# A two-layer graph attention kernel: the additive mask built by GpSimd during batch entry 0, and three moves in the hand-written order (seam transposes, queries, row normalization)

## The chip, the cores and the metric

One Trainium2 chip, one core of it. The metric is device time in microseconds (us) of one execution of the whole program; lower is better. Before the change it is 4377.3 us, the median of three runs (4373.14, 4377.3 and 4388.37).

## What is computed

The input `x` is 8 batch entries of 2048 nodes with 256 features, fp32; `adj` is one 2048 x 2048 int32 adjacency, shared by all entries. Two layers, each with a residual and a layer norm:

```
def _L0_gnn_ref(x, adj, prior, W, a_src, a_dst, beta_tilde, W_out):
    x_proj = jnp.einsum('bnd,hdf->bhnf', x, W)                 # 8 heads of 32
    e = leaky_relu(e_src[..., :, None] + e_dst[..., None, :], ALPHA)
    e = e + (beta * jnp.log(prior + EPS))[:, None, :, :]       # prior is adj
    e = jnp.where(adj > 0, e, neg_inf)
    h = softmax(e) @ x_proj ;  return h @ W_out.T
def _L1_gnn_ref(inp, adj, W1, W2, W3):
    e = leaky_relu((inp @ W1) @ (inp @ W2).T, ALPHA)
    e = jnp.where(adj > 0, e, NEG_INF)
    return relu(softmax(e) @ (inp @ W3))
x = _layernorm(x + _L0_gnn_ref(...)) ;  x = _layernorm(x + _L1_gnn_ref(...))
```

The mask of layer 1 (`where(adj > 0, e, NEG_INF)`) is applied as an addition: a bf16 tile `pen` is 0 where there is an edge and -3.0e38 where there is none.

## The kernel before

**Stages.** Layer 0 (class `Gat`, with `Unit` for one pair of heads and one half of the 2048 rows) is handled for batch entry 0 by itself: 4 head pairs x 16 steps, `g0.step(k)`, from the start to about 512 us. This stage is laid out by a scheduler, except on TensorE (PE), whose order is that of the program text. Its first 16 steps also make the matrix m = (adj + eps)^beta, masked: `make_m` (L199 to L209) loads an int32 block `adj_t` of 128 x 2048 (L203), and DVE (L205, L208) and ACT (L206, L207) turn it into `m`; TensorE transposes it and the result is stored in DRAM as `mt_d` (L214 to L222). All later uses load `mt_d` (L224). The projections of entries 1 to 7 are also interleaved with this stage.

From there on the order on all engines is written out by hand: `Stream` (L589) feeds the tiles of layer 0 of entry b while `Dot` (L666) does layer 1 of entry b-1. Its calls are `ahead` (ACT scales a tile, L478; DVE combines it, L492; GpSimd adds it up, L498) and `eat` (TensorE's products, L524). Between two entries lies a **seam** (L873 to L896): `rows(g)` (L401) projects the attention output (`y`, L409), adds the residual (L413) and takes statistics (L414); `rows_scale` (L416) computes the two layer-norm factors, `f[:,0]` on ACT (L420, L421) and `f[:,1]` = -mean * f[:,0] on DVE (L422); `rows_end` (L424) applies them on ACT (L429). `turn` (L437) then transposes the result x1 (`tr1`, L448; copied to SBUF as `x1t` by ACT, L449) and multiplies it by W3 (`h3p`, L454; copy L456). In `turn`, `lag` says how many pairs of 128-row blocks the h3 products stand behind the transposes: 1, and 4 in the last entry. At L882 to L885 the seam calls `stream.ahead(1)`, which at that place starts a new unit (two copies of `c` into PSUM on ACT, L488, and the first L492 of that unit), and then `next(turns)`.

After a seam come 16 **rows** of layer 1 (`Dot.step`, L705), each 128 nodes: scores `e` (L691), leaky relu `p` (L693), the mask and the row maximum in one DVE instruction (L700, reads `p` and `pen`), exp on ACT (L702), transposes `pt` (L718) and copies `pts` (L720), the product with h3 (`acc`, L742), relu on ACT (L743), residual `z` (L745), statistics (L747, L749). The layer norm of a row is finished one row later in `end_row` (L757): L762 and L763 give 1/std, L764 multiplies it on ACT by the negated mean (negated on DVE, L750), L765 scales `z`; then `store_row` stores it. Every fourth row `queries` (L675) makes the next four rows' left factor `h1` (`h1p`, L680; copies L682); it stands at the head of that row's step, ahead of its transposes. TensorE's small results share two PSUM buffers (`mm`).

**The mask.** `mask` (L229): for the rows of entry 0's layer 1 (it runs in the first streamed period, together with layer 0 of entry 1) the adjacency is loaded again, two int32 tiles `adj_r` of 128 x 1024 for each row (L237); DVE turns them into `pen` (L241), which is used and also stored in `pen_d` (L242). All later entries load `pen` from `pen_d` (L233).

The last entry's layer 1 (4069 us to the end) runs alone, with GpSimd idle.

Of the kernel before, what the change touches and what calls it, by code (L numbers as in the profile page):

```python
# [11 lines left out]
I32 = mybir.dt.int32  # L12
# [15 lines left out]
def kernel(  # L28
# [56 lines left out]
    def mm_tile(name):  # L85
        tag = banks[0]
        banks.append(banks.pop(0))
        if tag == "mm":
            return ps.tile([P, BK], F32, tag="mm", name=name)
        return pacc.tile([P, BK], F32, tag=tag, name=name)  # L90
# [7 lines left out]
    def ring_tile(name, shape=(P, N)):  # L98


        return wide.tile(list(shape), F32, tag="s", name=name, bufs=9)
# [97 lines left out]
    def make_m(n):  # L199

        rh, j2 = divmod(n, J2)
        a = wide.tile([P, NT // 2, 2 * P], I32, tag="d", name="adj_t", bufs=2)
        nc.sync.dma_start(a, adj[ts(rh, HALF), ts(j2, 2 * P)].rearrange("(t p) j -> p t j", p=P))  # L203
        m = ring_tile("m", (P, NT // 2, 2 * P))
        nc.vector.tensor_scalar(m, a, 0.0, None, ALU.max)  # L205
        nc.scalar.activation(m, m, AF.Ln, bias=eps_prior)  # L206
        nc.scalar.activation(m, m, AF.Exp, scale=beta_c)  # L207
        nc.vector.scalar_tensor_tensor(m, a, 0.0, m, ALU.is_gt, ALU.mult)  # L208
        return m  # L209
# [16 lines left out]
        nc.sync.dma_start(mt, mt_d[n, :, i])  # L226
        return mt

    def mask(it, make):  # L229

        pen = wide_tile("pen", "pen", 1, BF16)
        if not make:
            nc.sync.dma_start(pen, pen_d[ts(it, P), :])  # L233
            return pen, lambda: None
        edges = [chunk.tile([P, HALF], I32, tag="ht", name="adj_r", bufs=4) for _ in range(2)]
        for s, a in enumerate(edges):
            nc.sync.dma_start(a, adj[ts(it, P), ts(s, HALF)])  # L237

        def put():
            for s, a in enumerate(edges):  # L240
                nc.vector.tensor_scalar(pen[:, ts(s, HALF)], a, 0.0, NO_EDGE, ALU.is_le, ALU.mult)  # L241
            nc.sync.dma_start(pen_d[ts(it, P), :], pen)  # L242
        return pen, put

    def row_tile(name, bufs=4):
        return small.tile([P, D], F32, tag="row", name=name, bufs=bufs)
# [14 lines left out]
    class Gat:  # L261


        def __init__(self, b):
            self.b = b
            self.ms, self.mts, self.v = [], [], {}

        def begin(self):

# [131 lines left out]
        def rows(self, g):  # L401


            self.load_rows(g + 2)
            self.st = st = small.tile([P, IG // 2, nc.vector.BN_STATS_DIM], F32, name="st4", bufs=2)
            ys = [mm_tile("y").rearrange("p (t c) -> p t c", t=2) for _ in range(IG // 2)]
            for k in range(IG):
                for kc in range(KC):
                    nc.tensor.matmul(ys[k // 2][:, k % 2, :], self.ht[kc][:, ts(g * IG + k, P)], wot[:, kc, :],  # L409
                                     start=(kc == 0), stop=(kc == KC - 1))  # L410
            for k, y in enumerate(ys):
                z = self.x1(2 * g + k)
                nc.vector.tensor_add(z, y, self.xs[g][:, ts(k, 2), :])  # L413
                nc.vector.bn_stats(st[:, k, :], z.rearrange("p t c -> p c t"))  # L414

        def rows_scale(self):  # L416

            mv = self.st.rearrange("p a (t c) -> p (a t) c", t=2)
            self.f = f = small.tile([P, 2, IG], F32, name="f4", bufs=2)
            nc.scalar.activation(f[:, 0, :], mv[:, :, 2], AF.Ln, bias=eps_ln, scale=1.0 / D)  # L420
            nc.scalar.activation(f[:, 0, :], f[:, 0, :], AF.Exp, scale=-0.5)  # L421
            nc.vector.scalar_tensor_tensor(f[:, 1, :], mv[:, :, 1], -1.0, f[:, 0, :], ALU.mult, ALU.mult)  # L422

        def rows_end(self, g):  # L424

            for k in range(IG):
                z, f = self.x1(2 * g + k // 2), self.f
                row = z[:, k % 2, :]
                nc.scalar.activation(row, row, AF.Identity, bias=f[:, 1, k:k + 1], scale=f[:, 0, k:k + 1])  # L429
                if k % 2:  # L430
                    nc.scalar.dma_start(x1_d[self.b].rearrange("(t p) d -> p t d", p=P)[:, ts(2 * g + k // 2, 2), :], z)
# [5 lines left out]
        def turn(self):  # L437


            self.x1t = x1t = whole.tile([P, KC, N], F32, tag="x1t", name="x1t")  # L440
            self.h3 = h3 = whole.tile([P, NT, D], F32, tag="h3", name="h3")
            lag = 1 if self.b + 1 < B else 4
            for j in range(NT // 2 + lag):
                if j < NT // 2:
                    t = mm_tile("tr1")
                    for kc in range(KC):
                        for i in range(2):
                            nc.tensor.transpose(t[:, ts(kc * 2 + i, P)], self.x1(j)[:, i, ts(kc, P)], ident)  # L448
                    nc.scalar.copy(x1t[:, :, ts(j, 2 * P)], t.rearrange("p (k i) -> p k i", k=KC))  # L449
                if j >= lag:  # L450
                    t = mm_tile("h3p")
                    for i in range(2):
                        for kc in range(KC):
                            nc.tensor.matmul(t[:, ts(i, D)], x1t[:, kc, ts(2 * (j - lag) + i, P)], w3s[:, kc, :],  # L454
                                             start=(kc == 0), stop=(kc == KC - 1))
                    nc.scalar.copy(h3[:, ts(j - lag, 2), :], t.rearrange("p (i c) -> p i c", i=2))  # L456
                if j > 0:
                    yield
# [207 lines left out]
    class Dot:  # L666
# [16 lines left out]

        def scores(self, it, between=lambda c: None, after=lambda c: None):

            (pen, put), p = mask(it, self.b == 0), self.p
            for c in range(NB):
                between(c)
                t = mm_tile("e")
                for kc in range(KC):  # L690
                    nc.tensor.matmul(t, self.h1[:, kc, ts(it % IG, P)], self.x1t[:, kc, ts(c, BK)],  # L691
                                     start=(kc == 0), stop=(kc == KC - 1))
                nc.scalar.activation(p[:, ts(c, BK)], t, AF.Prelu, alpha=ALPHA)  # L693
                if c == 2:
                    put()
                if c < NB - 1:
                    after(c)
            neg = small.tile([P, 1], F32, name="neg")
            den = small.tile([P, 1], F32, name="den1")
            nc.vector.tensor_tensor_reduce(p, p, pen, -1.0, FMAX, ALU.add, ALU.min, neg)  # L700
            after(NB - 1)
            nc.scalar.activation(p, p, AF.Exp, bias=neg, scale=-1.0, accum_out=den)  # L702
            self.ahead = den

        def step(self, stream, count, lead=0):  # L705
# [16 lines left out]

            behind = count
            if it + 1 < NT:
                if (it + 1) % IG == 0:
                    self.queries((it + 1) // IG)
                self.scores(it + 1, turned, lambda c: stream.feed())
                behind -= NB
            else:
                for g in range(NB):  # L730
                    turned(g)
                stream.ahead()
                lead -= 1
            rec = small.tile([P, 1], F32, name="rec1", bufs=2)
            nc.vector.reciprocal(rec, den)
            self.end_row()
            stream.ahead(2 if it + 1 == NT else 1)
            acc = mm_tile("acc")[:, 0:D]
            for g in range(NB):
                for k in range(IG):  # L740
# [6 lines left out]
            nc.vector.bn_stats(st, z)  # L747
            f = small.tile([P, 4], F32, name="f", bufs=3)
            nc.vector.bn_aggr(f[:, 0:2], st)  # L749
            nc.vector.tensor_scalar(f[:, 0:1], f[:, 0:1], -1.0, None, ALU.mult)  # L750
            self.store_row()
            self.ended = it, z, f
            stream.eat(1)
            stream.ahead(behind - (2 if it + 1 == NT else 1) + lead)
            stream.eat(behind - 1)

        def end_row(self):  # L757


            if self.ended:  # L760
                it, z, f = self.ended
                nc.scalar.activation(f[:, 2:3], f[:, 1:2], AF.Ln, bias=eps_ln)  # L762
                nc.scalar.activation(f[:, 3:4], f[:, 2:3], AF.Exp, scale=-0.5)  # L763
                nc.scalar.activation(f[:, 2:3], f[:, 3:4], AF.Identity, scale=f[:, 0:1])  # L764
                nc.scalar.activation(z, z, AF.Identity, bias=f[:, 2:3], scale=f[:, 3:4])  # L765

        def store_row(self):
# [86 lines left out]
    for b in range(1, B + 1):  # L854
# [19 lines left out]
        for g in range(NB + 2):  # L874
            if g < NB:
                gat.rows(g)
            if g == 0 and dot:
                dot.end_row()
                dot.store_row()
            if 0 < g <= NB:  # L880
                gat.rows_end(g - 1)
            stream.eat(1)  # L882
            stream.ahead(1)
            if g > 1:
                next(turns)  # L885
            if g < NB:
                gat.rows_scale()
            if g < NB + 1:
# [14 lines left out]
    dot.step(stream, 0)  # L903
    dot.step(stream, 0)
    dot.end_row()
    dot.store_row()
# [1 line left out]
_INS = ['x', 'adj', 'L0_gnn_W', 'L0_gnn_a_src', 'L0_gnn_a_dst', 'L0_gnn_beta_tilde', 'L0_gnn_W_out',  # L908
# [27 lines left out]
```

## Time and profile before

| | |
|---|---|
| median of 3 runs | 4377.3 us |
| the profiled execution: its time | 4372.4 us |
| the profiled execution: its span | 4370.6 us |
| PE, DVE, ACT, POOL busy in the span | 4126.0, 3334.9, 2905.3, 2888.3 us |
| mean granted TensorE clock | 0.979 |

How to read it: the page lists busy time by engine, then 40 slices of the span, DMA queues, the chain of work that ended last, and groups of instructions by line. PE is TensorE's matmul side, PEld its weight loads, DVE is VectorE, ACT ScalarE, POOL GpSimd, SP the engine that issues most DMAs. A busy share is an average over stages with different limits, so the windows view, which gives busy time in chosen stretches, is more useful here. Where one period of the streamed part begins and ends is read from the first `y` product (L409) of each seam: 512.5, 1058.0, 1559.6, 2063.9, 2563.5, 3072.4, 3581.3 and 4069.0 us. The first `h1p` (L680), where the rows begin, is at 579.0, 1115.3, 1617.2, 2123.2, 2623.9, 3132.7, 3641.3 and 4095.2 us.

### The profile page before, as it was taken

The page shows a single profiled execution, that of the slowest core. Times are in us where ns is not written, and L with a number is a line of the kernel's source. Part 1 is how long each engine was busy: PE and PEld are TensorE (multiplying, and loading weights), DVE is VectorE, ACT ScalarE, POOL GpSimd, SP SyncE. Part 2 cuts the span into 40 slices and gives each one's busy share as a digit, 9 for nine tenths or more (in the row PEclk, how much of TensorE's full clock was granted, in tenths as well). Part 3 has the DMA queues.
Part 4 walks back from the last instruction along what each step waited for, and adds up shares of the span by engine and source line. Part 5 has one row for each costly group of instructions (what it writes and reads, how often), then busy time and mean ns, then how long its engine had stood idle before and what let it go on. Part 6 is the DMA issues. An engine that isn't in the chain of part 4 may idle for free.

```text
span 4370.6 us, 60300 instructions
## 1 busy us (share of the span) xinstructions
PE 4126.0 (94%) x22704; PEld 2090.3 (48%) x22704; DVE 3334.9 (76%) x3278; ACT 2905.3 (66%) x4132; POOL 2888.3 (66%) x1190
## 2 busy tenths in 40 slices
PE   7899799998999999999899999999899999999999
PEld 4444344444444444445444454444444444444766
DVE  7888788988878887788777887788787787787222
ACT  6422466676677767677777776677677776776555
POOL 0000477877788887889788877888687887888000
PEclk9999999999999999999999999999999999999999
DMA  8888755666565565556556564656555565554211
GB/s 268 275 288 285 237 198 196 218 223 218 184 198 189 188 205 191 178 195 215 186 178 203 195 207 166 193 193 197 190 199 180 186 219 171 187 192 158 79 46 46
DMA packets 346437, 843.63 MB, mean 193 GB/s; under 512 B 49696, under 2 KB 166432, under 8 KB 346144
## 3 DMA queue, kind: packets, MB, share of 16 engines
q1 hardware_dynamic: 328736, 822.99, 57.4%
q10 hardware_dynamic: 17408, 16.78, 1.1%
q8 instruction: 178, 2.92, 0.3%
q14 instruction: 115, 0.94, 0.1%
HBM read 763.76 MB, written 75.37 MB: 192 GB/s over the span
## 4 chain that ended last, share of the span: by engine, by line
PE 66%; ACT 12%; DVE 9%; issue 6%; DMA 5%; POOL 1%; SPq 1%; ACTq 0%; DVEq 0%; POOLq 0%
PE e L691 18%; PE val L524 15%; PE acc L742 14%; PE den L524 6%; PE pt L718 5%; ACT s L478 5%; DVE s L492 5%; DMA mt<-mt_d 3%; PE h3p L454 3%; DVE p L700 2%; PE h1p L680 2%; ACT p L702 2%; PE y L409 2%; ACT c L488 1%; PE proj L294 1%
## 5 line engine op out<-in xcount | busy, mean ns | idle before, releaser
L498 POOL TENSOR_TENSOR sums<-sums,s 128x1024 f32<-128x1024 f32 x1008 | 2505.7, 2523 | 272.8 <-DVE s L492 271.9
L492 DVE SCALAR_TENSOR_TENSOR s<-c,re,s 128x1024 f32<-128x1024 f32 x1232 | 1500.8, 1272 | 269.9 <-ACT c L488 197.6
L478 ACT ACTIVATE s<-mt,re 128x1024 f32<-128x1024 f32 x1232 | 1339.8, 1140 | 49.9 <-DMA mt<-mt_d 38.7
L524 PE MATMUL val<-s,v 128*32 128x512 f32 x8192 | 1094.5, 607 | 30.7 <-DVE s L492 17.8
L691 PE MATMUL e<-x1t,h 128*128 128x512 f32 x2048 | 995.8, 610 | 45.9 <-ACT pts L720 30.4
L742 PE MATMUL acc<-h,pts 128*128 128x256 f32 x4096 | 918.3, 382 | 1.5 <-ACT pts L720 1.0
L742 PEld LDWEIGHTS acc<-h,pts 128*128 128x128 f32 x4096 | 770.4, 190 | 198.5 <-ACT p L693 29.3
L700 DVE CUSTOM_DVE_ANT_0 p<-p,pen 128x2048 f32<-128x2048 f32 x128 | 459.6, 3591 | 310.3 <-ACT p L693 310.1
L492 DVE SCALAR_TENSOR_TENSOR s<-c,re,mt 128x1024 f32<-128x1024 f32 x560 | 687.5, 1268 | 0.0
L498 POOL TENSOR_TENSOR sums<-s 128x1024 f32<-128x1024 f32 x112 | 291.9, 2629 | 412.4 <-DVE s L492 405.1
L693 ACT ACTIVATE p<-e 128x512 f32<-128x512 f32 x512 | 306.8, 599 | 383.4 <-PE e L691 383.4
L524 PEld LDWEIGHTS val<-s,v 128*32 128x32 f32 x8192 | 203.1, 109 | 683.2 <-issue 442.9
L691 PEld LDWEIGHTS e<-x1t,h 128*128 128x128 f32 x2048 | 356.0, 194 | 333.9 <-issue 258.9
L702 ACT ACTIVATE p<-p,neg 128x2048 f32<-128x2048 f32 x128 | 256.5, 2004 | 374.2 <-DVE neg L700 373.6
L524 PE MATMUL den<-s,re 128*32 128x512 f32 x3264 | 443.1, 594 | 0.0
L718 PEld LDWEIGHTS pt<-ident,p 128*128 128x128 f32 x2048 | 224.1, 142 | 456.0 <-ACT p L693 129.1
L718 PE MATMUL pt<-ident,p 128*128 128x128 f32 x2048 | 332.7, 287 | 73.1 <-ACT p L702 39.5
L492 DVE SCALAR_TENSOR_TENSOR s<-c_in,re,mt 128x1024 f32<-128x1024 f32 x256 | 310.2, 1277 | 51.6 <-DMA mt<-mt_d 39.5
L720 ACT COPY pts<-pt 128x512 f32<-128x512 f32 x512 | 294.5, 579 | 79.8 <-PE pt L718 79.0
L305 POOL PARTITION_ALL_REDUCE top<-top x8 | 6.6, 821 | 428.9 <-DVE top L304 412.5
L524 PEld LDWEIGHTS den<-s,re 128*32 128x32 f32 x3264 | 110.1, 110 | 244.6 <-issue 242.9
L745 DVE TENSOR_TENSOR z<-acc,x1r 128x256 f32<-128x256 f32 x128 | 54.0, 422 | 199.0 <-ACT acc L743 189.8
(96 smaller groups left out, 2493.7 us busy)
## 6 DMA issues: line engine op xcount, KB each, us to landing
mt<-mt_d SPq DMA_DIRECT2D x992, 512.0 KB
c_in<-c_d SPq DMA_DIRECT2D x64, 1024.0 KB
pen<-pen_d SPq DMA_DIRECT2D x112, 512.0 KB
xg<-in_x_dram SPq DMA_DIRECT2D x60, 512.0 KB
adj_t<-in_adj_dram SPq DMA_DIRECT2D x16, 1024.0 KB
mt_d<-mt SPq DMA_DIRECT2D x32, 512.0 KB
rb<-rec_d SPq DMA_DIRECT2D x128, 128.0 KB
x_d<-ht ACTq DMA_DIRECT2D x64, 256.0 KB
```

The costliest lines, as they stand in the source:

```text
L454: nc.tensor.matmul(t[:, ts(i, D)], x1t[:, kc, ts(2 * (j - lag) + i, P)], w3s[:, kc, :], start=(kc == 0), stop=(kc == KC - 1))
L478: nc.scalar.activation(s[:, a], mt, AF.Copy, scale=self.gat.re[:, 1, jt, h:h + 1])
L492: nc.vector.scalar_tensor_tensor(s[:, a], self.c[a], self.gat.re[:, 0, jt, h:h + 1], m, ALU.max, ALU.mult)
L498: nc.gpsimd.tensor_tensor(self.sums[:, a], of[:, a], s[:, a], ALU.add)
L524: nc.tensor.matmul(dst[ts(q, DH), :], weights[q % 2], s[:, q % 2, ts(q // 2, BK)], start=start, stop=stop)
L691: nc.tensor.matmul(t, self.h1[:, kc, ts(it % IG, P)], self.x1t[:, kc, ts(c, BK)], start=(kc == 0), stop=(kc == KC - 1))
L693: nc.scalar.activation(p[:, ts(c, BK)], t, AF.Prelu, alpha=ALPHA)
L700: nc.vector.tensor_tensor_reduce(p, p, pen, -1.0, FMAX, ALU.add, ALU.min, neg)
L702: nc.scalar.activation(p, p, AF.Exp, bias=neg, scale=-1.0, accum_out=den)
L718: nc.tensor.transpose(t[:, ts(k, P)], p[:, ts(g * IG + k, P)], ident)
L720: nc.scalar.copy(pt, t)
L742: nc.tensor.matmul(acc, pts[g][:, ts(k, P)], self.h3[:, j, :], start=(j == 0), stop=(j == NT - 1))
```

## The change

1. **Mask.** `make_m` now also makes the mask from the block it has loaded: GpSimd writes `pen_t` (128 x 2048, bf16) from `adj_t`, and SP stores it to `pen_d`. This happens 16 times, in the first 16 steps. `mask` only loads `pen`; L237, L241 and L242 are gone.
2. **Seam.** `rows_scale` no longer issues L422; `rows_factor` does, called in the next `rows` after both residual adds and ahead of their statistics (and in `rows_end`). The two adds now stand ahead of the two statistics. `next(turns)` comes ahead of `stream.ahead(1)`, and `lag` is 2 instead of 1.
3. **Queries.** `queries` is called near the end of the step before, after the first `eat` that follows `acc`, ahead of the remaining `ahead` calls.
4. **Row normalization.** L750 and L764 are gone. A new `end_mean` computes -mean/std in one DVE instruction from two SBUF operands and then issues the ACT scaling of `z`; it is called after `stream.ahead(...)`, so that ACT's scalings of the next tile stand ahead of it, and the relu (L743) stands behind it.

```diff
@@ make_m
         nc.sync.dma_start(a, adj[ts(rh, HALF), ts(j2, 2 * P)].rearrange("(t p) j -> p t j", p=P))
+        pen = wide.tile([P, NT // 2, 2 * P], BF16, tag="c", name="pen_t", bufs=1)
+        nc.gpsimd.tensor_scalar(pen, a, 0.0, NO_EDGE, ALU.is_le, ALU.mult)
+        nc.sync.dma_start(pen_d[ts(rh, HALF), ts(j2, 2 * P)].rearrange("(t p) j -> p t j", p=P), pen)
         m = ring_tile("m", (P, NT // 2, 2 * P))
@@ mask
-    def mask(it, make):
+    def mask(it):
         pen = wide_tile("pen", "pen", 1, BF16)
-        if not make:
-            nc.sync.dma_start(pen, pen_d[ts(it, P), :])
-            return pen, lambda: None
-        edges = [chunk.tile([P, HALF], I32, tag="ht", name="adj_r", bufs=4) for _ in range(2)]
-        for s, a in enumerate(edges):
-            nc.sync.dma_start(a, adj[ts(it, P), ts(s, HALF)])
-        def put():
-            for s, a in enumerate(edges):
-                nc.vector.tensor_scalar(pen[:, ts(s, HALF)], a, 0.0, NO_EDGE, ALU.is_le, ALU.mult)
-            nc.sync.dma_start(pen_d[ts(it, P), :], pen)
-        return pen, put
+        nc.sync.dma_start(pen, pen_d[ts(it, P), :])
+        return pen
@@ Gat.rows, rows_scale, rows_end, turn
                 nc.vector.tensor_add(z, y, self.xs[g][:, ts(k, 2), :])
-                nc.vector.bn_stats(st[:, k, :], z.rearrange("p t c -> p c t"))
+            self.rows_factor()
+            for k in range(len(ys)):
+                nc.vector.bn_stats(st[:, k, :], self.x1(2 * g + k).rearrange("p t c -> p c t"))
...
-            nc.vector.scalar_tensor_tensor(f[:, 1, :], mv[:, :, 1], -1.0, f[:, 0, :], ALU.mult, ALU.mult)
+        def rows_factor(self):
+            if self.mv is not None:
+                nc.vector.scalar_tensor_tensor(self.f[:, 1, :], self.mv[:, :, 1], -1.0, self.f[:, 0, :], ALU.mult, ALU.mult)
+                self.mv = None
         def rows_end(self, g):
+            self.rows_factor()
...
-            lag = 1 if self.b + 1 < B else 4
+            lag = 2 if self.b + 1 < B else 4
@@ Dot.scores: (pen, put), p = mask(it, self.b == 0), self.p  becomes  pen, p = mask(it), self.p
-                if c == 2:
-                    put()
@@ Dot.step, end_row, and the new end_mean
             if it + 1 < NT:
-                if (it + 1) % IG == 0:
-                    self.queries((it + 1) // IG)
                 self.scores(it + 1, turned, lambda c: stream.feed())
...
             stream.ahead(2 if it + 1 == NT else 1)
+            self.end_mean()
             acc = mm_tile("acc")[:, 0:D]
...
-            nc.vector.tensor_scalar(f[:, 0:1], f[:, 0:1], -1.0, None, ALU.mult)
...
             stream.eat(1)
+            if (it + 2) % IG == 0 and it + 2 < NT:
+                self.queries((it + 2) // IG)
             stream.ahead(behind - (2 if it + 1 == NT else 1) + lead)
...
-                nc.scalar.activation(f[:, 2:3], f[:, 3:4], AF.Identity, scale=f[:, 0:1])
+        def end_mean(self):
+            if self.ended:
+                it, z, f = self.ended
+                nc.vector.scalar_tensor_tensor(f[:, 2:3], f[:, 0:1], -1.0, f[:, 3:4], ALU.mult, ALU.mult)
                 nc.scalar.activation(z, z, AF.Identity, bias=f[:, 2:3], scale=f[:, 3:4])
@@ the seam loop (end_mean is also called after each other end_row)
             stream.eat(1)
-            stream.ahead(1)
             if g > 1:
                 next(turns)
+            stream.ahead(1)
```

More of the change, by code (lines that the diff above doesn't have):

```diff
@@ L265, in __init__ @@
             self.b = b
-            self.ms, self.mts, self.v = [], [], {}
+            self.ms, self.mts, self.v, self.mv = [], [], {}, None
         def begin(self):
@@ L413, in rows @@
                 nc.vector.tensor_add(z, y, self.xs[g][:, ts(k, 2), :])
-                nc.vector.bn_stats(st[:, k, :], z.rearrange("p t c -> p c t"))
+            self.rows_factor()
+            for k in range(len(ys)):
+                nc.vector.bn_stats(st[:, k, :], self.x1(2 * g + k).rearrange("p t c -> p c t"))
         def rows_scale(self):
-            mv = self.st.rearrange("p a (t c) -> p (a t) c", t=2)
+            self.mv = mv = self.st.rearrange("p a (t c) -> p (a t) c", t=2)
             self.f = f = small.tile([P, 2, IG], F32, name="f4", bufs=2)
@@ L684, in scores @@
         def scores(self, it, between=lambda c: None, after=lambda c: None):
-            (pen, put), p = mask(it, self.b == 0), self.p
+            pen, p = mask(it), self.p
             for c in range(NB):
@@ L878 @@
                 dot.end_row()
+                dot.end_mean()
                 dot.store_row()
@@ L905 @@
     dot.end_row()
+    dot.end_mean()
     dot.store_row()
```

## The prediction

> **What bounds the kernel now.** First the page: busy time by engine, and the 40 slices (one is 109 us).
>
> ```profile
> PE 4126.0 (94%) x22704; PEld 2090.3 (48%) x22704; DVE 3334.9 (76%) x3278; ACT 2905.3 (66%) x4132; POOL 2888.3 (66%) x1190
> ...
> PE   7899799998999999999899999999899999999999
> ...
> DVE  7888788988878887788777887788787787787222
> ...
> POOL 0000477877788887889788877888687887888000
> ```
>
> TensorE is near full, so only its 4370.6 - 4126.0 = 244.6 us of idle time can be won. GpSimd is idle for the first four slices. Then the windows view (us; busy us and count of PE, PEld, DVE, ACT, POOL; clock; DMA share; GB/s):
>
> ```profile
> 35.60:175.00 139.40, 119.67 (x868) 68.94 (x870) 128.23 (x99) 101.59 (x106) 0.37 (x1) 0.95 0.82 277
> ...
> 579.00:1058.00 479.00, 442.55 (x2321) 210.61 (x2320) 421.54 (x384) 325.71 (x446) 384.33 (x154) 0.97 0.65 215
> ...
> 1115.30:1559.60 444.30, 429.43 (x2322) 206.60 (x2321) 357.35 (x348) 324.62 (x441) 372.69 (x152) 0.99 0.60 192
> ```
>
> In the stretch that makes `m` (35.6 to 175) DVE, not PE, is the fullest: 128.2 of 139.4 us. Later PE bounds. The 16 rows with the masks (579 to 1058) take 479.0 us. Next, what PE waited for in one ordinary period (1559.6 to 2061):
>
> ```profile
> PE pt L718 <- ACT p L702: 6.2, 1, 6.2
> PE h3p L454 <- ACT x1t L449: 5.5, 1, 5.5
> PE e L691 <- ACT pts L720: 5.0, 1, 5.0
> ...
> PE pt L718 <- ACT h L682: 1.5, 1, 1.5
> PE e L691 <- DVE z L745: 0.9, 1, 0.9
> ```
>
> These five are 19.1 us of 21.9 idle. Last, single lines (count: shortest/median/longest ns). L700 reads two SBUF tiles: first in the last stage, where GpSimd rests, then in the six periods where it works; L422, two small SBUF operands, likewise; then L750 (one operand) and L498, GpSimd's usual instruction.
>
> ```profile
> L700 DVE CUSTOM_DVE_ANT_0 p<-p,pen x16: 2291/2292/2293, 4106.4 to 4349.7; 128x2048 f32<-128x2048 f32 x16
> L700 DVE CUSTOM_DVE_ANT_0 p<-p,pen x95: 2605/3555/7764, 1131.1 to 4032.1; 128x2048 f32<-128x2048 f32 x95
> L422 DVE SCALAR_TENSOR_TENSOR f<-st,f x4: 161/162/165, 4075.7 to 4089.0; 128x4 f32<-128x4 f32 x4
> L422 DVE SCALAR_TENSOR_TENSOR f<-st,f x28: 161/1012/3859, 526.0 to 3625.7; 128x4 f32<-128x4 f32 x28
> L750 DVE TENSOR_SCALAR f<-f x128: 153/154/155, 633.7 to 4366.2; 128x1 f32<-128x1 f32 x128
> L498 POOL TENSOR_TENSOR sums<-sums,s x1008: 2337/2380/4482, 491.7 to 4039.2; 128x1024 f32<-128x1024 f32 x168
> ```
>
> Read them together: a DVE instruction with two SBUF operands waits while GpSimd works, one with a single operand does not. In the timeline L422 at 1099.71 ends at 1101.04, just when GpSimd's instruction ends (1098.64 + 2.34). This row prices two of the four parts.
>
> **The change, part by part** (minus is time won).
>
> *A. Entry 0's rows lose the masks: -33 us.* Gone are 32 L241 (70.3 us of DVE, mean 2.23), 32 loads of `adj_r` and 16 stores with their places in SP's queue; 16 loads of `pen` come instead. The rows of the next five periods, from first `h1p` to the next seam, take 444.3, 446.7, 440.3, 448.6 and 448.6, mean 445.7. 479.0 - 445.7 = 33.3. Next late is PE itself, as there. Bounds -25 to -37.
>
> *B. Stage 0 gains 16 GpSimd instructions: +24.* No row shows this instruction. Below: a GpSimd memset writes 128 columns in 205 ns and one column in 100, so 0.82 ns a column, 1.7 us for 2048. Above: two L498, 4.8 us. I take one L498, 2.4 us: it reads 2 x 1024 elements, as many as this one. GpSimd is free, but DVE isn't: L205, L208, L326 and L492 of this stretch (here `c` lies in SBUF) are of the kind that waits, or move two elements a cycle (L205: 2048 in 1.22 us). Two of the 16 fall before 35.6, where DVE rests. 14 x 2.4 = 34; DVE's 11.2 idle us of the stretch cover that much, 22 stay, and PE, which eats what DVE makes, ends as much later. SP: 16 stores of 512 KB, 8.4 MB, 30 us at the 277 GB/s of the row, against 0.18 x 139 = 25 us of idle queues plus the 22 new ones: covered. At the start GpSimd's first mask stands ahead of L305, and a third `adj_t` load, which waits for a buffer, now ahead of the store `c_d` on the way to the first L492: +2. Bounds: 0 (GpSimd uses only gaps) to 14 x 4.8 + 2 = +69.
>
> The Trainium skill, page "GPSIMD Engine Reference", section 3.1, gives one-input loops of few operations 1.03 cycles an element at 1.2 GHz: an estimate of 1.8 us, by which B would be about +16 and the sum about -24.
>
> *C. Seven seams: -3 each, -21.* Today PE stands from 1076.47 to 1081.59, since the `x1t` copies are queued behind two `c` copies (0.98 each) and two L478 (1.1 each), and h3's first product needs them. Then it runs cold: 8 matmuls in 3.78 us instead of 1.89. Now the copies go first (1.1 us) and h3 isn't asked for yet; but the next in PE's order is the new unit's first `val`, which needs L492, which needs `c`, and `c` is 1.1 us later: L492 from 1079.1, `val` from 1080.4 and in full from 1081.6. So the wait stays and only changes its name; won is 1 us, and one h3 product (1.9 us) that moves behind the scores into the 6.2 us that PE waits for the first exp. L422 behind the adds costs nothing: it waited for ACT 14 times, 3 us each, and does so later. Bounds: -5.5, and +1 if the new wait of part E at a seam's start delays ACT's scalings.
>
> *D. Queries earlier: -12.* PE waited 13.8 us in seven periods for `h` ahead of a transpose and 3.5 ahead of scores; two `val` groups now lie in between. I take two thirds. Bounds 0 and -17.
>
> *E. `end_mean`: +26.* Per row DVE loses L750 (0.15) and gets an instruction of L422's kind. L700's rows price its wait: mean over the 112 busy rows (459.6 - 16 x 2.29) / 112 = 3.78, so 1.48 above 2.29. 112 x 1.48 = 166 us more DVE work, 24 in a period of 502 where DVE has 100 free. ACT loses L764 (0.29 x 128). Behind the waiting instruction on DVE is the residual add L745, on ACT L765 and behind it the relu, unit copies and `pts`, for which PE waits. In one row per period (the fourth) a new unit's `c` copies and four L492 (4.86 us) stand ahead of it: there DVE would reach `end_mean` at 1779.8 instead of ACT finishing `z` at 1775.0, GpSimd is in an instruction until 1781.1, the relu goes from 1778.9 to 1782.0, and PE's 5.0 us wait for `pts` grows by 3: 7 x 3 = +21. In the other rows the relu comes about 1 us later; PE wants that buffer 4.2 us after `acc`, so only long waits show: +5. Bounds 0 and +40 for the two.
>
> The Trainium skill, page "SBUF — State Buffer", section "Who interferes with whom", speaks against B and E: DVE and GpSimd share one port pair as an exclusive lock for a whole instruction, two-operand DVE instructions contend with any GpSimd instruction that reads SBUF. The rows of L422, L700 and L750 agree (161 against 1012 ns; 154 always).
>
> **Sum:** -33 + 24 - 21 - 12 + 26 = **-16 us**. On the profiled execution, 4372.4 us (span 4370.6 and 1.8 around it), that is 4356; it lies 4.9 below the median shown, on whose scale I say **4360**.
>
> **Rivals** (median scale).
> - *Cheap GpSimd, no held row:* B +13, E1 0, seams -28. -16 - 11 - 21 - 7 = -55: 4322. For it: most PE waits in the row are short. Against: the L422 row.
> - *GpSimd as the new bound of stage 0:* its instruction takes 4.8 us, two L498. B is +69, sum +29: 4406, slower. It decides from about 3.5 us (B = +40, sum 0). For: DVE at 128 of 139. Against: one operand read, not two.
> - *`end_mean` in place of the removed wait:* L745 frees one of PE's two small buffers; in the row at 1823 it ends 1.6 us ahead of need, and L422 waited up to 3.7. If half of 112 rows lose 1.2 us, +67: 4428. For: in entry 0, where DVE was late, PE waited for L745 6.4 us, not 0.9.
> - *The seam changes the name of its wait only:* C is 0: 4382, no change.
>
> **Chances.** Forecast 0.37 (0.27 faster by over 0.3%, which is 13 us and about what this measurement tells from none; 0.10 within), first rival 0.18, second 0.20, third 0.15, fourth 0.10 (0.06 within, 0.04 slower). Faster 0.45, within 0.16, slower 0.39. The range leaves out part of the third and the best of the first: 4310 to 4425; the forecast's own is 4345 to 4378.
>
> **What would show it.** A: rows of entry 0 near 446 us instead of 479. B: the start of the first seam, 512.5 now, near 537; DVE's L492 in stage 0 longer than 1.28 us; the GpSimd instruction's mean. C: PE's wait at h3p gone, one at `val` for L492 in its place, 21 us less over seven seams. D: waits for `h` gone. E: `end_mean` near 1.6 us, PE's `pts` wait in the fourth row near 8. Wrong if GpSimd's instruction is far from 2.4 us, or if DVE isn't held by it.

## The result and the profile after

The changed kernel takes **4532.1 us** (median of four runs, 4524.5 to 4534.0) against 4379.2 for the kernel before (4373.1 to 4388.4): ratio 1.0344, 95% interval 1.0322 to 1.0366. That is 151 us slower by the ratio (153 by the two medians). The forecast was 4360, its range ended at 4425, and the sign was wrong. The profiled execution spans 4532.1 us, 161.5 more than before's.

First the page of the changed kernel: busy times, and the slices of PE and GpSimd.

```profile
PE 4188.9 (92%) x22704; PEld 2097.7 (46%) x22704; DVE 3445.5 (76%) x3246; ACT 2859.4 (63%) x4004; POOL 3060.3 (68%) x1206
...
PE   5689979999899999999899999999899999999999
...
POOL 4420157888788877888788877788777886788100
```

GpSimd now works in the first slices, and there PE has holes (5, 6, 8) where it had 7, 8, 9. The windows view of the same kernel (columns as before) for the stretch that makes `m`, and for the rows of entry 0:

```profile
35.60:175.00 139.40, 85.43 (x486) 51.03 (x484) 96.80 (x49) 62.69 (x60) 74.29 (x9) 0.77 0.58 187
698.30:1150.90 452.60, 433.76 (x2330) 207.81 (x2329) 373.85 (x348) 321.83 (x429) 378.83 (x153) 0.99 0.58 190
```

In the same 139.4 us PE does 486 products instead of 868 and DVE 49 instructions instead of 99; even the transfers fall from 277 to 187 GB/s. No engine is full: this is a chain of waits. The rows of entry 0 did get shorter, 452.6 instead of 479.0.

By the first `y` of each seam the 161.5 us split without a rest: stage 0 632.3 instead of 512.5 (+119.8), the first streamed period 518.6 instead of 545.5 (-26.9), the next six periods 7 to 15 us longer each (+66.1), the rest +2.5. What PE waits for in one ordinary period (1662.8 to 2178), the longest four:

```profile
PE e L692 <- DVE z L743: 6.8, 4, 3.2
PE val L525 <- DVE s L493: 6.6, 2, 6.2
PE pt L717 <- ACT pts L719: 6.4, 4, 2.9
PE h1p L681 <- DVE z L743: 4.5, 3, 2.3
```

Before's waits for `p`, for `x1t` ahead of `h3p` and for `h` are gone; in their place stand a `val` (a product of `eat`) that waits for DVE, and two lines that wait for `z`, the residual add behind the new `end_mean`. Single lines of the changed kernel, shortest/median/longest ns:

```profile
L205 POOL TENSOR_SCALAR pen_t<-adj_t x16: 7132/8130/12387, 18.3 to 264.8; 128x2048 bf16<-128x2048 int32 x16
L769 DVE SCALAR_TENSOR_TENSOR f<-f x128: 142/2100/4733, 771.6 to 4528.1; 128x1 f32<-128x1 f32 x128
```

I had taken 2.4 us for the first and some 1.6 for the second. The second was right (mean 1.67); the first is 8.5 on average. How a slow mask holds the stage is seen in the timeline of the changed kernel, first GpSimd's, then SP's queue:

```profile
71.92 8.12 POOL L205 TENSOR_SCALAR pen_t<-adj_t 128x2048 bf16<-128x2048 int32 x1 [8.42 <-DMA adj_t<-in_adj_dram]
87.75 8.12 POOL L205 TENSOR_SCALAR pen_t<-adj_t 128x2048 bf16<-128x2048 int32 x1 [7.70 <-DMA adj_t<-in_adj_dram]
```

```profile
80.07 0.37 SPq L206 DMA_DIRECT2D pen_d<-pen_t  x1
80.76 0.38 SPq L203 DMA_DIRECT2D adj_t<-in_adj_dram  x1
```

The mask ends at 80.04; its store is issued at 80.07; only behind the store can SP issue the next load (80.76), which lands at 87.7, when the next mask starts. Mask, store and load stand in a row, 16 us a tile, and DVE and ACT wait for the same load. How much of the 120 us the order of the queue makes is tested below (e9). Beside this, one DVE product L493, begun at 73.02 while the mask runs, takes 5.51 us; over the stage they take 1499 ns on average instead of 1277.

### The profile page after: what moved, and what is told of

Same layout as the page of the kernel before. It is cut to its first block, busy times and chain, and to the rows that moved or that the text cites. A ratio compares the mean times of both kernels' runs of the same rounds, so it can differ in the third digit from the quotient of the medians.

```text
span 4532.1 us, 60131 instructions
## 1 busy us (share of the span) xinstructions
PE 4188.9 (92%) x22704; PEld 2097.7 (46%) x22704; DVE 3445.5 (76%) x3246; ACT 2859.4 (63%) x4004; POOL 3060.3 (68%) x1206
## 4 chain that ended last, share of the span: by engine, by line
PE 57%; DVE 16%; ACT 9%; issue 8%; DMA 3%; POOL 1%; ACTq 1%; SPq 0%; DVEq 0%; POOLq 0%
PE e L692 18%; PE val L525 13%; PE acc L740 10%; DVE s L493 10%; PE pt L717 5%; PE den L525 5%; ACT s L479 3%; DVE f L769 3%; DMA mt<-mt_d 2%; PE h1p L681 2%; DVE p L699 2%; PE proj L287 1%; ACT c L489 1%; PE y L402 1%; ACT ht L430 1%
## 5 line engine op out<-in xcount | busy, mean ns | idle before, releaser
L499 POOL TENSOR_TENSOR sums<-sums,s 128x1024 f32<-128x1024 f32 x1008 | 2534.3, 2547 | 313.2 <-DVE s L493 310.7
L493 DVE SCALAR_TENSOR_TENSOR s<-c,re,s 128x1024 f32<-128x1024 f32 x1232 | 1500.8, 1271 | 319.2 <-ACT c L489 227.0
L525 PE MATMUL val<-s,v 128*32 128x512 f32 x8192 | 1149.9, 614 | 140.8 <-DVE s L493 130.8
L493 DVE SCALAR_TENSOR_TENSOR s<-c,re,mt 128x1024 f32<-128x1024 f32 x560 | 687.4, 1268 | 0.0
L699 DVE CUSTOM_DVE_ANT_0 p<-p,pen 128x2048 f32<-128x2048 f32 x128 | 407.0, 3180 | 330.6 <-ACT p L694 330.6
L525 PE MATMUL den<-s,re 128*32 128x512 f32 x3264 | 464.4, 602 | 0.0
L493 DVE SCALAR_TENSOR_TENSOR s<-c_in,re,mt 128x1024 f32<-128x1024 f32 x256 | 367.6, 1499 | 52.2 <-DMA mt<-mt_d 41.3
L770 ACT ACTIVATE z<-z,f 128x256 f32<-128x256 f32 x128 | 76.8, 600 | 290.4 <-DVE f L769 290.4
L769 DVE SCALAR_TENSOR_TENSOR f<-f 128x1 f32<-128x1 f32 x128 | 213.5, 1668 | 41.6 <-ACT f L762 40.7
```

The lines of the kernel that those rows point to most:

```text
L493: nc.vector.scalar_tensor_tensor(s[:, a], self.c[a], self.gat.re[:, 0, jt, h:h + 1], m, ALU.max, ALU.mult)
L499: nc.gpsimd.tensor_tensor(self.sums[:, a], of[:, a], s[:, a], ALU.add)
L525: nc.tensor.matmul(dst[ts(q, DH), :], weights[q % 2], s[:, q % 2, ts(q // 2, BK)], start=start, stop=stop)
L769: nc.vector.scalar_tensor_tensor(f[:, 2:3], f[:, 0:1], -1.0, f[:, 3:4], ALU.mult, ALU.mult)
```

## The experiments

"+84 us" means the ratio to the kernel before, times its median in the same runs. "First y" is the start of the first seam in the one profiled execution, 512.5 before; the seven other kernels with before's stage 0 (e2, e3, e5 to e8, e12) had 511.8 to 520.1, so 8 us there mean nothing. My theory: the slow mask makes the 120 us, the mean's product the +10 a period. Rivals: the seams or the queries cost something; SP's queue and the buffers, not GpSimd's time, hold stage 0; and for the mean, ScalarE's order rather than VectorE's wait.

### The change in two halves

**e1: the mask alone** (A and B of the prediction, item 1 of the diff).

> The kernel before with part A and B alone: the mask made by GpSimd in stage 0, no mask work in entry 0's rows; seams, queries and mean as before. Theory 1 (the 16 GpSimd instructions of 8.5 us hold stage 0, the rest of the change costs some 10 us a period): first y of period 1 near 632 us as in the changed kernel (before 512.5), entry 0's rows some 26 to 33 us shorter than before's 479.0, every later period as before, so +87 to +94 us, about 4470 us. Rival (the whole loss is the mask, and the later periods lose through what it leaves behind): about 4530 us. Rival (the seams and queries disturb stage 0 as well): first y clearly under 632 us.

Measured: 1.0192 (1.0159 to 1.0224), +84 us. First y 627.9; entry 0's rows 445.9 (-33.1); the later periods as before.

**e2: all but the mask** (C, D and E: items 2, 3 and 4).

> The changed kernel with before's mask (made by VectorE in entry 0's rows): seams, queries and mean are changed, the mask is not. Theory 1: stage 0 as before (first y near 512.5 us), the six streamed periods some 10 us longer each, so +55 to +70 us, about 4440 us. Rival (the loss is the mask alone): 4379 us or less.

Measured: 1.0180 (1.0158 to 1.0203), +79 us; six periods 6 to 17 us longer. The halves add up to 163 of 151 us: they are two separate losses.

**e3: the mean alone** (E, item 4).

> The kernel before with part E alone: the row's mean is negated and scaled on VectorE behind the next products, so that ScalarE's scaling of the row stands behind it. Theory 1 (the mean's product, held by GpSimd, and ScalarE's scaling and relu behind it cost the rows): +60 to +90 us, more than all but the mask together, since seams and queries give some of it back. Rival (the mean is as cheap as predicted and the queries' earlier place costs the 10 us a period): +10 to +30 us here.

Measured: 1.0221 (1.0193 to 1.0249), **+97 us**. So the second half is part E, and seams and queries give some back. The timeline of one row of this kernel shows how; the lines are L498 (GpSimd's sums), L770 (the mean), L771 (scaling of z), L744 (relu), L746 (residual add):

```profile
3041.61 4.72 POOL L498 TENSOR_TENSOR sums<-sums,s 128x1024 f32<-128x1024 f32 x2
...
3044.18 2.17 DVE L770 SCALAR_TENSOR_TENSOR f<-f 128x1 f32<-128x1 f32 x1
...
3046.38 0.60 ACT L771 ACTIVATE z<-z,f 128x256 f32<-128x256 f32 x1 [2.32 <-DVE f L770]
3047.00 0.45 ACT L744 ACTIVATE acc<-acc,rec 128x256 f32<-128x256 f32 x1
...
3047.48 0.43 DVE L746 TENSOR_TENSOR z<-acc,x1r 128x256 f32<-128x256 f32 x1 [1.14 <-ACT acc L744]
...
3047.96 1.45 PE L691 MATMUL e<-x1t,h 128*128 128x512 f32 x2 [2.86 <-DVE z L746]
```

One number a partition takes DVE 2.17 us, until GpSimd's two sums end (3041.61 + 4.72 = 3046.33). Then z, relu and add follow one by one, and only the add frees PE's buffer: PE stands 2.86 us. In the kernel before PE waited 0.90 us at the same place (2980.49).

Over six periods (3084.7 us against 3011.0) PE's idle time grows by 38.6 us. `e` behind `z` is 46.7 us instead of 5.7 (18 times instead of 6), transposes behind `h` 28.4 instead of 9.7; gone are 23.6 us of `e` behind `pts`. But PE's busy time grows too, by 35.1 us for the same 15,637 instructions: the granted clock is 0.97 instead of 0.98 there. The clock records of its trace have PE at half speed for 184 us instead of 113, and half of the difference is 36. All 33 half-speed stretches of e3 (17 in the kernel before), each 3.4 to 10.2 us long, begin within a stop of PE of 2.8 us or more or at most 1.2 us behind its end: such a stop is paid a second time. The Trainium skill, page "TensorE: Matmul & The Clock Gate", Part 1, says that the clock falls to half after an idle window of about 3.4 us; here stops of 2.8 us were enough.

### The mean: wait or place

**e7: the same step with one tensor operand.**

```diff
-nc.vector.scalar_tensor_tensor(f[:, 2:3], f[:, 0:1], -1.0, f[:, 3:4], ALU.mult, ALU.mult)
+nc.vector.tensor_scalar(f[:, 2:3], f[:, 0:1], f[:, 3:4], -1.0, ALU.mult, ALU.mult)
```

> Part E alone as in the run with the mean only (+96 us), but the product on VectorE takes one tensor and two scalars, one of them per partition, in place of two tensors. If GpSimd's hold of the two-operand instruction is the cause, it falls from 1.9 us median to about 0.2 and the time to +10 to +50. If the place of the step is the cause (VectorE and ScalarE reach it only behind the new unit's copies and products), the duration falls and the time stays at +70 to +100.

Measured: 0.9991 (0.9977 to 1.0005), -4 us. All 97 us are gone, more than I expected. The line in this kernel:

```profile
L770 DVE TENSOR_SCALAR f<-f x128: 195/199/215, 658.1 to 4365.1; 128x1 f32<-128x1 f32 x128
```

The same place, engine and values, about ten times as fast (median 1886 ns in e3): what cost the time is that DVE reads two SBUF tensors while GpSimd works.

**e8: the place alone.** The negation on DVE (L750 of before) stays, and `end_mean` computes the product as before did, on ScalarE.

```diff
-nc.vector.scalar_tensor_tensor(f[:, 2:3], f[:, 0:1], -1.0, f[:, 3:4], ALU.mult, ALU.mult)
+nc.scalar.activation(f[:, 2:3], f[:, 3:4], AF.Identity, scale=f[:, 0:1])
```

> Part E's place alone: the three small ScalarE instructions and the negation stay as before, but the last small one and the scaling of z come behind the next scalings and products, where the changed kernel has them. If VectorE's late product is the cause of +96, it falls to 0 to +25. If ScalarE's order (z and the relu behind the unit's copies and scalings) is the cause, it stays at +60 or more.

Measured: 0.9974 (0.9959 to 0.9989), **-11 us**. ScalarE's order isn't the cause; behind the next scalings is even the better place for the scaling of z. In the profiled executions this gain lies in the first streamed period (534.3 us instead of 545.5), and the six later ones take as long as before (3010.8 and 3011.0 us).

### Seams and queries

**e5: part C alone** (item 2).

> The kernel before with part C alone: at the seams the transposes of x1 ahead of the scalings, h3's products two pairs later, the row factor's product behind the adds. My forecast's term: -21 us. Rival (the wait changes its name only): 0. The mean alone cost +96 and everything but the mask +80, so seams and queries together should be worth some -16: I expect -5 to -15 here, and the seams themselves (first y to first h1p) no shorter than before's 57 to 60 us by more than 3.

Measured: 0.9980 (0.9967 to 0.9993), -9 us. The wait changed its name, as the fourth rival said. In this kernel at one seam (2500 to 2660), where before had 5.5 us of `h3p` behind `x1t`:

```profile
PE val L532 <- DVE s L500: 7.1, 2, 6.8
```

Still it gains: the seams are 0 to 3 us longer, but the rows that follow, with one `h3p` more to fill their first wait, are 2 to 9 us shorter in six of seven periods. From the first seam to the last, PE's idle time falls from 185.5 us (3556.5 - 3371.0) to 163.5 (3540.2 - 3376.7); its busy time grows by 5.7. Over all seven seams PE waits 53.1 us at `val` where it had waited 40.4 at `h3p`, but the rows' wait for `p` falls from 39.5 us to 0.9.

**e6: part D alone** (item 3).

> The kernel before with part D alone: the queries of the next four rows come one row step earlier, behind the residual add. My forecast's term: -12 us, by the waits of PE for h ahead of a transpose that go. Rival (the queries now take the small buffers right behind acc, so PE waits there for z's add: that wait was 31 us in the changed kernel): 0 to +15. I expect -12 to 0.

Measured: 1.0003 (0.9988 to 1.0018), +1 us. The gain was given back. From the first seam to the last PE's 13.8 us behind `h` are gone, but `h1p` now waits 7.7 us for the buffer that z's add frees, `pt` behind `pts` 24.4 instead of 19.6, `pt` behind `p` 44.1 instead of 39.5, against 26.9 instead of 30.4 for `e` behind `pts`: -13.8 + 7.7 + 4.8 + 4.6 - 3.5 = -0.2.

### The mask in stage 0

**e4: on VectorE**, with the same buffers and queue.

```diff
-        nc.gpsimd.tensor_scalar(pen, a, 0.0, NO_EDGE, ALU.is_le, ALU.mult)
+        nc.vector.tensor_scalar(pen, a, 0.0, NO_EDGE, ALU.is_le, ALU.mult)
```

> Parts A and B with VectorE in place of GpSimd: the mask is made in stage 0 from the same tile, one instruction for each of the 16, with the same buffers and the same store in the same queue. Theory 1 (GpSimd's 8.5 us are what holds stage 0): the instruction takes 1.3 to 2.1 us, stage 0 grows by 10 to 35 us, entry 0's rows lose 26 to 33 us, so the total is -20 to +10 us, 4360 to 4390 us. Rival (the second reader of the tile, the one buffer and the store in the queue ahead of the next loads hold stage 0, whatever engine makes the mask): first y still 60 us or more late, above 4420 us.

Measured: 1.0007 (0.9991 to 1.0024), +3 us. The instruction takes 1.22 us, first y 543.6 (+31.1), entry 0's rows 454.6 (-24.4). With the same buffers and queue, three quarters of GpSimd's +115 are gone.

**e9, e10, e11: the store from GpSimd's queue**, with the mask on GpSimd, VectorE and ScalarE.

```diff
-        nc.sync.dma_start(pen_d[...]..., pen)
+        nc.gpsimd.dma_start(pen_d[...]..., pen)
# e11, the mask itself:
+        nc.scalar.activation(pen, a, AF.Copy, bias=NO_EDGE, scale=-NO_EDGE)
```

> The mask alone made by GpSimd (as in the run that cost +84 us), with one edit more: its store is issued from GpSimd's own queue instead of SP's. In that run the loads of adj_t stood behind the stores in SP's queue, so that a mask, its store and the next load came one after the other, some 16 us a tile. Theory Q (this chain is what holds stage 0): the load comes while the mask before it is made, a tile takes 8.5 to 11 us, the first y comes at 535 to 575 instead of 628, and the total is -10 to +30 us against before. Theory L (GpSimd's 8.1 us and its hold of VectorE are what costs): the first y stays above 600, the total above +55 us.

> The mask made by VectorE in stage 0 (it cost +4 us with the store in SP's queue: stage 0 +31, entry 0's rows -25), with the store from GpSimd's queue. Theory Q: the loads of adj_t are no longer held, stage 0 is +10 to +20 us (16 instructions of 1.22 us are 19.6), the total -20 to -5 us. Theory L: the store's queue doesn't matter, stage 0 stays +31 and the total 0 to +8 us.

> The mask made by ScalarE in stage 0 (one Copy with scale and bias, exact for edges of 0 and 1), its store from GpSimd's queue. ScalarE is busy 101.6 of the 139.4 us in which the stage makes m, and a pass over 2048 columns takes it some 2 us: 16 of them are 32 us, against 38 idle. If VectorE's fullness was what its mask cost, stage 0 is +0 to +15 us and the total -30 to -10 us; if any engine's mask costs its own time, +25 to +35 and 0.

Measured: e9 1.0146 (1.0123 to 1.0169), +64 us, first y 605.6; e10 1.0016 (1.0003 to 1.0030), +7 us, 555.8; e11 0.9965 (0.9948 to 0.9982), **-15 us**, 537.1 (+24.6) with entry 0's rows at 441.2. SP's queue holds the loads for 22 us of GpSimd's 115, not for all of it. The masks themselves don't come faster: the 16 start from 18.7 to 262.6 us in e9 and from 18.4 to 264.8 in e1, some 16 us a tile, since in e9 the next one waits until the store has emptied the single buffer `pen_t`:

```profile
POOL pen_t L205 <- DMA pen_d<-pen_t: 74.3, 13, 9.0
```

For VectorE the queue is not what counts, against my expectation. ScalarE's mask (1.91 us each) costs stage 0 24.6 us and wins 37.8 in the rows.

**e12: prices.** In the last stage, where GpSimd rests, nine of its instructions over 128x2048, twice, with results that nothing uses.

> The kernel before, and in its last stage, where GpSimd rests, two rounds of nine GpSimd instructions over 128x2048 whose results go nowhere. It prices the instruction that I took for 2.4 us and that took 8.1. If the conversion from integers is what is slow, the forms from int32 take about 8 us and those from f32 2 to 5. If the two operations are slow, the forms with one take half. If GpSimd takes a fixed time for an element, all with one input take about 8 us, and the product of two tensors (4.8 by the row of the sums) is an exception.

Four of the nine in this kernel; L908 is the change's own instruction, L911 the same from f32, L913 one product, L916 product and sum:

```profile
L908 POOL TENSOR_SCALAR price_h<-price_a x2: 7082/7113/7144, 4101.4 to 4154.3; 128x2048 bf16<-128x2048 int32 x2
L911 POOL TENSOR_SCALAR price_h<-price_f x2: 7083/7084/7084, 4121.1 to 4174.3; 128x2048 bf16<-128x2048 f32 x2
L913 POOL TENSOR_SCALAR price_g<-price_f x2: 5373/5378/5382, 4135.3 to 4188.5; 128x2048 f32<-128x2048 f32 x2
L916 POOL TENSOR_SCALAR price_g<-price_f x2: 1899/1899/1899, 4152.4 to 4204.7; 128x2048 f32<-128x2048 f32 x2
```

None of my three readings holds. Types don't matter (7.08 to 7.40 us from int32, f32 or bf16). One operation costs 5.37 us, a comparison and a product 7.08, but a product and a sum 1.90: the choice of operations decides, by a factor of 3.7. The Trainium skill, page "GPSIMD Engine Reference", section 3.1, has 1.03 cycles an element for up to two operations, by my estimate 1.8 us; the last row agrees, the other three are three to four times as long.

**e13, e14: the mask by product and sum**, from SP's queue and from GpSimd's.

```diff
-        nc.gpsimd.tensor_scalar(pen, a, 0.0, NO_EDGE, ALU.is_le, ALU.mult)
+        nc.gpsimd.tensor_scalar(pen, a, -NO_EDGE, NO_EDGE, ALU.mult, ALU.add)
```

> Parts A and B with one instruction changed: GpSimd's mask by mult and add in place of is_le and mult (exact for edges of 0 and 1), 1.9 us in the run of prices instead of 8.1. If the duration is what held stage 0, the first y comes at 525 to 545 (512.5 before, 627.9 with the slow form), which is my forecast's +24 give or take, entry 0's rows lose 25 to 33, and the total is -20 to +5 us. If the place in the queue or the hold of VectorE counts whatever the duration, the first y stays above 560 and the total above +20.

> As the run before, with the store from GpSimd's queue. If SP's queue still holds the next load by the mask's 1.9 us and the store, this gains 5 to 15 us on it; if GpSimd's own queue costs as much (its issues took 0.94 to 1.3 us each, and the one buffer waits 3.4 us for the store), it is the same within 5.

Measured: e13 1.0036 (1.0020 to 1.0052), +16 us, first y 568.1; e14 0.9997 (0.9985 to 1.0010), -1 us, first y 546.3. In e13:

```profile
L205 POOL TENSOR_SCALAR pen_t<-adj_t x16: 1887/2928/4135, 18.3 to 203.8; 128x2048 bf16<-128x2048 int32 x16
```

The instruction takes 2.9 us (median; at its shortest 1.89, as in e12), about what I had forecast, and stage 0 is still +55.6, with the first y above the 560 that I had set for a rival. By the prediction's sum 2.9 us would give +31. So a right price would not have saved the term. The queue is again 22 us.

**e17, e18: the mask without its store, the store without a mask.** Before's own masks stay; e17 adds e13's GpSimd instruction with an unused result, e18 adds 16 stores of 512 KB of `m` from GpSimd's queue to a place that nobody reads.

```diff
# e18, behind the last instruction of make_m:
+        nc.gpsimd.dma_start(more_d[...]..., m[:, :, 0:P])
```

> The kernel before, its own masks untouched, with GpSimd's mult-and-add over the 16 tiles of stage 0 added, whose result is not stored and not used. If the stores are what the remaining 25 to 34 us are, the first y stays within 8 us of 512.5 and the total within 10 us of before. If the instruction is, by its hold of VectorE and of the tile (14 in the stretch by 2.9 us), the first y is +20 to +35.

> The kernel before, its own masks untouched, with 16 more stores of 512 KB in stage 0, in the packets that the mask's store has, of part of m, from GpSimd's queue, to a place that nobody reads. If the stage is bound by its transfers (0.82 to 0.85 of the queues' time, 277 to 282 GB/s), 8.4 MB are 30 us: the first y is +20 to +32. If they fit in what the queues have free, as I forecast, +0 to +8.

Measured: e17 1.0063 (1.0044 to 1.0082), +28 us, first y 548.2 (+35.7); e18 1.0035 (1.0018 to 1.0053), +15 us, 537.2 (+24.7). Neither is free, and both together with the same queue (e14) cost +33.8 in first y: they overlap, so my two readings did not exclude each other. The 24.7 of e18 is the less certain: the execution that was profiled, 4407.7 us, lies 20 above the median, which gives the 15. DVE's product up to 215 us, in the kernel before and in e17:

```profile
L492 DVE SCALAR_TENSOR_TENSOR s<-c_in,re,mt 128x1024 f32<-128x1024 f32 x87 | 106.1, 1276 | 17.8 <-DMA c_in<-c_d 8.1 <-DMA mt<-mt_d 8.0 <-ACT mt L220 1.7
L494 DVE SCALAR_TENSOR_TENSOR s<-c_in,re,mt 128x1024 f32<-128x1024 f32 x69 | 97.6, 1467 | 14.4 <-ACT v L298 9.8 <-DMA mt<-mt_d 2.9 <-ACT mt L222 1.7
```

In e17 it takes 1467 ns on average instead of 1276, with no store at all; that is GpSimd's hold. In e18 it stays at 1277, and the loads come later (DVE waits 17.5 us for `adj_t` instead of 9.0) while from 35.6 to 175 us the queues move 301 GB/s instead of 277.

### Together

**e15: the changed kernel with two instructions replaced** (e13's mask, e7's mean).

> The changed kernel with two instructions replaced: the mask by mult and add, the mean's product with one tensor operand. If these two make the whole difference between forecast and result, the sum of the parts measured alone holds: seams -9, queries 0, mean 0, mask -20 to +5, so -30 to 0 us against before, some 4345 to 4375 us. If the parts disturb one another (queries and mean at the same small buffers), +10 to +40.

Measured: 1.0005 (0.9992 to 1.0019), +2 us. The single runs add up (16 - 9 + 1 - 4 = +4). Two lines of the change, written with other operations, make up all but 2 of its 151 us.

**e16: seams, e8's mean and e11's mask; queries as before.**

> The parts that gained alone: seams (-9 us), the mean on ScalarE behind the next scalings (-11), the mask on ScalarE with its store from GpSimd's queue (-15); the queries stay as before. If they add up, -35 us, about 4337 us; if seams and mean gain by the same waits, -20 to -28.

Measured: 0.9925 (0.9910 to 0.9941), **-33 us**, 4344.1 us: faster than both kernels (-9 - 11 - 15 = -35).

## Why the prediction was wrong, point by point

- **A, entry 0's rows: -33. Right.** 445.9 instead of 479.0 in e1. What was late next was PE, as said.
- **B, stage 0: +24 (bounds 0 to +69). Wrong, the largest miss: +115.** The failed step is "I take one L498, 2.4 us: it reads 2 x 1024 elements, as many as this one". The mask's instruction takes 8.1. Its own row was not in the trace, and even my upper end, 4.8, was too low: I priced by elements read, and the pair of operations decides. The second rival had the sign and was too small by the same error; but GpSimd is not the full engine that it named (74.3 busy of 139.4 us): it holds the others in chains of waits. From 8.1 to 2.9 us a mask the runs give back 60 us (627.9 to 568.1).
- **B's second failed step** is "SP: ... covered" and the "+2" for loads behind the stores. I counted the queue's bytes, not its order: each store waits for its mask, and each load of the next tile stands behind it. That is 22 us in both forms. And the bytes were not covered either: the stores alone cost 15 us, 24.7 in the profiled execution (e18). DVE's 11.2 idle us were no cover, since the instruction alone costs 36 (e17).
- **C, seams: -21. Right mechanism, too large: -9 (-14 to -3); -16 from first to last seam in the profiled execution.** The term that was mis-sized is "won is 1 us" at the seam itself: the new wait for `val` is longer than the one for `h3p` that went (53.1 us against 40.4 over seven seams), and only the h3 product's share, the rows' wait for `p`, is won.
- **D, queries: -12. Wrong: 0.** The waits for `h` went, but I named nothing that is late next: `h1p` itself, behind `z`, and then `p` and `pts` (e6). In the changed kernel, where `z` is later, `h1p` behind `z` is 27.0 us over six periods (3.6 in e3).
- **E, end_mean: +26 (bounds 0 to +40). Wrong: +97.** DVE's instruction was right (mean 1.67 us, forecast near 1.6). Failed is "PE wants that buffer 4.2 us after `acc`, so only long waits show: +5", and the +21 of the fourth row: there PE's six stops sum to 22.8 us in e3 and were 23.6 before. The loss came at other rows, with `e` behind `z` three times a period and not once, and half of it as half-speed time of PE, which I had not priced at all for this part though I had for the seam. The third rival named this wait (L745 frees the buffer); its +67 lacked the clock.
- **One reading was too wide:** "one with a single operand does not" wait. It rests on L750, which has one element a partition. L241 of the kernel before reads one tensor:

```profile
L241 DVE TENSOR_SCALAR pen<-adj_r x32: 677/2005/7612, 588.7 to 1023.5; 128x1024 bf16<-128x1024 int32 x32
```

The five of 677 to 695 ns are those beside which GpSimd rests; each of the others ends some 0.6 us behind the end of a GpSimd instruction that had begun before it or while it waited. So a larger instruction with one tensor can be held as well. (It is the form of L205, which the prediction counts among those that wait or move two elements a cycle.)

What stays open: why one operation on GpSimd takes longer than a product and a sum; no run tells. How the 34 us of e14 split between hold and stores isn't settled, since each alone costs as much. How the 93 us that the slow form still costs in e9 split between the hold on VectorE, the later release of `adj_t` and the wait for `pen_t` isn't known either: a second buffer for `pen_t` was not tried.

## What to carry to other kernels

Before an instruction goes to GpSimd beside a busy VectorE, run that very pair of operations once: the count of elements doesn't price it. A small VectorE instruction on a path that others wait for should read one SBUF tensor only, since with two it may take as long as what GpSimd has begun, or longer when GpSimd's instructions follow one another (L700: 7.76 us instead of 2.29). And a store can delay the loads issued behind it by the time of what it stores (22 us here with GpSimd's masks, nothing with VectorE's): look at the order in the queue, not at its share of busy time.

## What was not expected of the hardware

- GpSimd over 128x2048 (e12): one operation 5.37 us, comparison and product 7.08 whatever the types, product and sum 1.90.
- A scalar per partition from SBUF is no second operand in the sense of the wait: 195 to 215 ns with GpSimd busy, against 144 to 2181 for the form with two tensors. The Trainium skill, page "SBUF — State Buffer", section "Who interferes with whom", says that a VectorE instruction with at most one SBUF input, outside the 2-port perf modes, does not contend with GpSimd; the row agrees and extends this to a scalar operand.
- PE's stops cost nearly twice their length in e3: 38.6 us more idle, 35.1 more busy.
